# Recurrent feed-forward layer of a small graph network: transposed rows leave PSUM in copies of two tiles instead of four

## The chip, the cores and the metric

The kernel runs on one core of a Trainium2 chip. The metric is the time of one execution on the device, in microseconds (us), taken as the median of several runs. The engines are named as in the profile: PE is TensorE's matmul, PEld its loading of weights, DVE is VectorE, ACT is ScalarE, POOL is GpSimd, SP issues DMAs.

## The reference

The program is two layers over 3327 rows of 256 features: a graph attention, a mixture of 16 experts, a second graph attention and, last, a recurrence. The change is in the recurrence alone. Cut to it, the reference is:

```python
def step(h, _):
    h = h + 0.01 * jnp.tanh(h)
    h = h * jax.nn.sigmoid(h)
    h = _layernorm(h, ln_w, ln_b)
    h = jnp.einsum('bsc,dc->bsd', h, W) + b
    return (h, None)
x, _ = jax.lax.scan(step, x, None, length=N_ITERS)   # N_ITERS = 30
```

The state that the scan starts from is the normalized output of the second attention, and its result is added to that output.

## The kernel before

The rows stand in SBUF as 26 tiles of 128 rows by 256 features in float32, in one tensor `x`. The layers before the recurrence are not touched by the change. They end at 1106 us of the span; the recurrence is the rest.

A step goes over seven groups of tiles: groups 0 to 5 have four tiles each (G = 4), group 6 has two. For one group of n tiles the code issues, in this order:

- ACT: `th` = tanh of the state (L997).
- POOL: `th` = `th` + state (L999); the state is kept scaled by S = 100, which absorbs the factor 0.01.
- ACT: `z` = silu of `th` (L1000).
- DVE: the statistics of `z`, one instruction a tile (L1005), and their combination (L985); POOL: two small instructions that make the inverse deviation `rr` (L987, L988).
- PE: two transposes a tile (L1007) turn `z` into `pt`, a PSUM tile of the pool ps3t with two buffers.
- ACT: one copy of the whole of `pt` into `zT` in SBUF (L1009): 128x1024 for four tiles, 128x512 for the two of group 6.
- PE: two matmuls a tile (L1013) multiply `zT` by the matrix `wc` into `po`, a PSUM tile of the pool ps3o, also with two buffers. The profile shows each of these matmuls as two passes of 128x256: 4 passes a tile, 16 for a group of four tiles, 8 for group 6.
- DVE: the next state from `po`, `rr` and the bias, one instruction a tile (L1018), written into `x`.

So a step has 52 transposes and 104 passes of products. In the last step the group is also added to rows that were kept in DRAM (L1025, after a DMA load, L1024) and written out (L76).

The order of instructions on each engine is not that of the code. The framework's scheduler places them when the program is built, subject to data, to buffers coming free (`th`, `z`, `zT`, `pt` and `po` have two buffers each) and to its own estimates; each engine then works through its list in order and waits on semaphores. On PE the list before has this for a step (counts of instructions; a prime marks the next step):

```
pt x8 group 0, pt x8 group 1 | po x8 group 0, po x8 group 1
pt x8 group 2, pt x8 group 3 | po x8 group 2, po x8 group 3
pt x8 group 4, pt x8 group 5 | po x8 group 4, po x8 group 5
pt x4 group 6, pt x6 group 0' | po x4 group 6
```

The first row of the next step then begins with the two transposes of group 0' that are left. So the groups go in pairs, and group 6 goes by itself.

Of the kernel before, what the change touches and what calls it, by code (L numbers as in the profile page):

```python
# [30 lines left out]
def gat_moe_gat_recurrent_ffn(ctx: ExitStack, tc: tile.TileContext, a: dict, out: bass.AP):  # L31
    nc = tc.nc
# [40 lines left out]
    def move_pairs(dram, tile, c0, c1, into_dram):  # L73

        def move(dst, src):
            nc.sync.dma_start(*((dst, src) if into_dram else (src, dst)))  # L76

        full = min(c1, PAIRS - 1)
        if full > c0:
            move(  # L80
                dram[c0 * 2 * P : full * 2 * P, :].rearrange("(t p b) d -> p t (b d)", p=P, b=2),
                tile[:, : 2 * (full - c0), :].rearrange("p (t b) d -> p t (b d)", b=2),
            )
        if c1 == PAIRS:
            base, last = (PAIRS - 1) * 2 * P, 2 * (PAIRS - 1 - c0)
            for r0, r1 in spread(REST // 2):
                move(
                    dram[base + 2 * r0 : base + 2 * r1, :].rearrange("(p b) d -> p (b d)", b=2),
                    tile[r0:r1, last : last + 2, :].rearrange("p b d -> p (b d)"),
                )  # L90
            if REST % 2:
                move(dram[base + REST - 1 : base + REST, :], tile[REST // 2 : REST // 2 + 1, last, :])
# [882 lines left out]
    with ExitStack() as st:  # L975
        ps_t = st.enter_context(tc.tile_pool(name="ps3t", bufs=2, space=PSUM))
        ps_o = st.enter_context(tc.tile_pool(name="ps3o", bufs=2, space=PSUM))
        last_p = st.enter_context(tc.tile_pool(name="last", bufs=2))

        def inv_norm(stats, n):  # L980


            v = small.tile([P, G, 2], F32, name="v")
            for j in range(n):
                nc.vector.bn_aggr(v[:, j, :], stats[:, j, :])  # L985
            r = small.tile([P, G], F32, name="rr")
            nc.gpsimd.tensor_scalar(r[:, :n], v[:, :n, 1], EPS, None, op0=ALU.add)  # L987
            nc.gpsimd.tensor_tensor(r[:, :n], r[:, :n], neg_half[:, :n], ALU.pow)  # L988
            return r

        for step in range(N_STEPS):
            for ts in groups:
                n = len(ts)
                hs = x[:, ts[0] : ts[0] + n, :]
                th = steps.tile([P, G, D], F32, name="th")
                z = steps.tile([P, G, D], F32, name="z")
                nc.scalar.activation(th[:, :n, :], hs, AF.Tanh, scale=1.0 / S)  # L997

                nc.gpsimd.tensor_tensor(th[:, :n, :], th[:, :n, :], hs, ALU.add)  # L999
                nc.scalar.activation(z[:, :n, :], th[:, :n, :], AF.Silu, scale=1.0 / S)  # L1000
                stats = small.tile([P, G, 6], F32, name="stats")
                pt = ps_t.tile([P, G, KD, P], F32, name="pt")
                zT = steps.tile([P, G, KD, P], F32, name="zT")
                for j in range(n):
                    nc.vector.bn_stats(stats[:, j, :], z[:, j, :])  # L1005
                    for k in range(KD):
                        nc.tensor.transpose(pt[:, j, k, :], z[:, j, k * P : (k + 1) * P], ident)  # L1007
                rr = inv_norm(stats, n)
                nc.scalar.copy(zT[:, :n, :, :], pt[:, :n, :, :])  # L1009
                po = ps_o.tile([P, G, D], F32, name="po")  # L1010
                for j in range(n):
                    for k in range(KD):
                        nc.tensor.matmul(  # L1013
                            po[:, j, :], lhsT=zT[:, j, k, :], rhs=wc[:, k, :],
                            start=(k == 0), stop=(k == KD - 1),
                        )
                for j in range(n):
                    nc.vector.scalar_tensor_tensor(  # L1018
                        x[:, ts[0] + j, :], po[:, j, :], rr[:, j : j + 1], bb, op0=ALU.mult, op1=ALU.add
                    )  # L1020
                if step == N_STEPS - 1:
                    here = slice(ts[0] * P, (ts[-1] + 1) * P)
                    old = last_p.tile([P, G, D], F32, name="old")
                    nc.sync.dma_start(old[:, :n, :], kept[here, :].rearrange("(t p) d -> p t d", p=P))  # L1024
                    nc.vector.scalar_tensor_tensor(  # L1025
                        hs, hs, 1.0 / S, old[:, :n, :], op0=ALU.mult, op1=ALU.add
                    )
                    move_pairs(out, hs, ts[0] // 2, (ts[-1] + 1) // 2, True)
# [49 lines left out]
```

## Time and profile before

| | before |
|---|---|
| median of 7 runs | 2012.43 us (2010.3 to 2014.83) |
| the profiled execution's own time | 2012.6 us |
| span of its profile | 2010.9 us |
| PE busy | 1935.0 us (96%) |
| DVE, ACT, POOL busy | 1299.5 us (65%), 1095.9 us (54%), 952.7 us (47%) |
| granted TensorE clock, mean | 0.993 |
| recurrence in the span | 1106 us to the end |

The profile is of one execution. A busy engine is one with an instruction under way; the instructions of PE overlap, so the distance from one start to the next says more of its rate than the duration of one. An idle time stands beside what ended it. In the timeline, equal instructions that follow each other without a gap are one row with a count.

### The profile page before, as it was taken

The page shows a single profiled execution, that of the slowest core. Times are in us where ns is not written, and L with a number is a line of the kernel's source. Part 1 is how long each engine was busy: PE and PEld are TensorE (multiplying, and loading weights), DVE is VectorE, ACT ScalarE, POOL GpSimd, SP SyncE. Part 2 cuts the span into 40 slices and gives each one's busy share as a digit, 9 for nine tenths or more (in the row PEclk, how much of TensorE's full clock was granted, in tenths as well). Part 3 has the DMA queues.
Part 4 walks back from the last instruction along what each step waited for, and adds up shares of the span by engine and source line. Part 5 has one row for each costly group of instructions (what it writes and reads, how often), then busy time and mean ns, then how long its engine had stood idle before and what let it go on. Part 6 is the DMA issues. An engine that isn't in the chain of part 4 may idle for free.

```text
span 2010.9 us, 33554 instructions
## 1 busy us (share of the span) xinstructions
PE 1935.0 (96%) x12032; PEld 1752.0 (87%) x12032; DVE 1299.5 (65%) x3847; ACT 1095.9 (54%) x1419; POOL 952.7 (47%) x870
## 2 busy tenths in 40 slices
PE   7999999999999987999999999999999999999998
PEld 6999999989999986888888888888888888888887
DVE  6887887722222215667676777777777777777777
ACT  2966766621111114567555666666666666666664
POOL 3020212443333324001000777877887787787785
PEclk9999999999999998999999999999999999999999
DMA  8977141199999854000000000000000000000003
GB/s 165 119 99 117 15 72 49 50 303 321 348 326 310 299 171 137 8 9 16 9 16 11 25 1 1 1 1 1 1 1 1 1 1 1 1 1 1 1 1 115
DMA packets 139755, 157.08 MB, mean 78 GB/s; under 512 B 52028, under 2 KB 99365, under 8 KB 139587
## 3 DMA queue, kind: packets, MB, share of 16 engines
q1 hardware_dynamic: 123466, 122.05, 19.5%
q0 software_dynamic: 11440, 28.09, 8.2%
q10 hardware_dynamic: 4680, 4.76, 0.7%
q8 instruction: 98, 1.61, 0.3%
q14 instruction: 71, 0.57, 0.1%
HBM read 164.58 MB, written 29.78 MB: 97 GB/s over the span
## 4 chain that ended last, share of the span: by engine, by line
PE 68%; issue 10%; POOL 5%; ACT 5%; DVE 4%; DMA 2%; another core or an unknown queue 0%; SPq 0%; POOLq 0%; DVEq 0%; ACTq 0%
PE po L1013 35%; PE acc L262 23%; PE pt L1007 5%; ACT zT L1009 5%; POOL given L831 2%; POOL rb L730 2%; DVE pT L257 2%; PE bank L786 2%; DMA given<-wh,to 2%; PE acc L827 1%; PE bank L499 1%; PE bank L221 1%; DMA zT<-given 0%; POOL rstd L120 0%
## 5 line engine op out<-in xcount | busy, mean ns | idle before, releaser
L1013 PE MATMUL po<-wc,zT 128*128 128x256 f32 x3120 | 706.0, 383 | 21.7 <-ACT zT L1009 21.1
L1013 PEld LDWEIGHTS po<-wc,zT 128*128 128x128 f32 x3120 | 583.4, 190 | 124.5 <-ACT zT L1009 49.9
L262 PE MATMUL acc<-wh,pT 128*128 128x129 f32 (+1 forms) x4056 | 606.4, 310 | 3.2 <-DVE pT L257 3.1
L262 PEld LDWEIGHTS acc<-wh,pT 128*128 128x128 f32 x4056 | 561.2, 191 | 41.4 <-DVE pT L257 4.8
L252 ACT ACTIVATE e<-rb,minus,full 128x384 f32<-128x384 f32 (+3 forms) x494 | 400.2, 824 | 182.0 <-DVE pT L257 163.6
L999 POOL TENSOR_TENSOR th<-th,x 128x1024 f32<-128x1024 f32 (+1 forms) x210 | 460.9, 2215 | 63.9 <-ACT th L997 63.9
L257 DVE SCALAR_TENSOR_TENSOR pT<-e,part,adjT 128x384 f32<-128x384 f32 (+3 forms) x494 | 380.3, 774 | 138.3 <-PE acc L262 120.7
L1018 DVE SCALAR_TENSOR_TENSOR x<-po,rr,bb 128x256 f32<-128x256 f32 x780 | 324.9, 477 | 118.3 <-PE po L1013 113.9
L1009 ACT COPY zT<-pt 128x1024 f32<-128x1024 f32 (+1 forms) x210 | 199.0, 948 | 333.9 <-PE pt L1007 333.9
L1005 DVE BATCH_NORM_STATS2 stats<-z 128x6 f32<-128x256 f32 x780 | 283.7, 415 | 117.5 <-ACT z L1000 117.5
L120 POOL TENSOR_TENSOR rstd<-ve,neg_half 128x4 f32<-128x4 f32 (+3 forms) x28 | 30.0, 1072 | 405.5 <-DVE ve L118 316.0
L988 POOL TENSOR_TENSOR rr<-rr,neg_half 128x4 f32<-128x4 f32 (+1 forms) x210 | 208.0, 990 | 17.4
L1000 ACT ACTIVATE z<-th 128x1024 f32<-128x1024 f32 (+1 forms) x210 | 210.7, 1003 | 0.5 <-POOL th L999 0.5
L997 ACT ACTIVATE th<-x 128x1024 f32<-128x1024 f32 (+1 forms) x210 | 199.4, 996 | 1.9 <-DVE x L127 0.9
L1007 PE MATMUL pt<-ident,z 128*128 128x128 f32 x1560 | 191.0, 274 | 2.5 <-DVE high L943 2.5
L1007 PEld LDWEIGHTS pt<-ident,z 128*128 128x128 f32 x1560 | 178.8, 142 | 14.8 <-issue 2.9
L820 DVE TENSOR_TENSOR pT<-e,bank 128x512 f32<-128x512 f32 x61 | 41.9, 687 | 182.8 <-PE bank L786 122.1
L786 PEld LDWEIGHTS bank<-hT,wh 128*128 128x128 f32 x1280 | 150.7, 194 | 8.1 <-issue 3.4
L786 PE MATMUL bank<-hT,wh 128*128 128x128 f32 x1280 | 151.9, 277 | 5.5 <-issue 3.0
L816 ACT ACTIVATE e<-bank 128x512 f32<-128x512 f32 x61 | 36.4, 597 | 194.6 <-issue 91.3
L831 POOL DMA_INDIRECT given<-wh,to x61 | 60.2, 987 | 167.7 <-DVE wh L830 148.6
L565 POOL DMA_INDIRECT lists<-pair,ati x52 | 62.5, 1202 | 134.7 <-DVE ati L552 44.0
(189 smaller groups left out, 1241.8 us busy)
## 6 DMA issues: line engine op xcount, KB each, us to landing
wh<-in_w_dram SPq DMA_DIRECT2D x120, 512.0 KB
first_set<-in_w_dram SPq DMA_DIRECT2D x63, 512.0 KB
in_bytes<-in_adj_dram POOLq DMA_DIRECT2D x3, 2496.0 KB
x<-in_x_dram SPq DMA_DIRECT2D x6, 512.0 KB
kept<-x SPq DMA_DIRECT2D x8, 384.0 KB
old<-kept SPq DMA_DIRECT2D x6, 512.0 KB
out_dram<-x SPq DMA_DIRECT2D x6, 512.0 KB
table_x<-row ACTq DMA_DIRECT2D x3, 768.0 KB
```

The costliest lines, as they stand in the source:

```text
L252: nc.scalar.activation(e[:, : n * P], rb[:, : n * P], AF.Relu, scale=sc.full[:, j, h : h + 1], bias=sc.minus[:, j, h : h + 1],)
L257: masked = nc.vector.scalar_tensor_tensor(pT[:, : n * P], e[:, : n * P], sc.part[:, j, h : h + 1], adjT[:, j // 2, ts[0] * P : (ts[-1] + 1 ...
L262: nc.tensor.matmul(po[c], lhsT=pT[:, c * P : (c + 1) * P], rhs=wh[:, j, h, :], start=(j == 0 and c % per_bank == 0), stop=(j == NT - 1), s ...
L786: nc.tensor.matmul(p[:, f, :], lhsT=w[:, k, f * P : (f + 1) * P], rhs=hT[:, k, :], start=(k == 0), stop=(k == KD - 1),)
L988: nc.gpsimd.tensor_tensor(r[:, :n], r[:, :n], neg_half[:, :n], ALU.pow)
L999: nc.gpsimd.tensor_tensor(th[:, :n, :], th[:, :n, :], hs, ALU.add)
L1000: nc.scalar.activation(z[:, :n, :], th[:, :n, :], AF.Silu, scale=1.0 / S)
L1005: nc.vector.bn_stats(stats[:, j, :], z[:, j, :])
L1007: nc.tensor.transpose(pt[:, j, k, :], z[:, j, k * P : (k + 1) * P], ident)
L1009: nc.scalar.copy(zT[:, :n, :, :], pt[:, :n, :, :])
L1013: nc.tensor.matmul(po[:, j, :], lhsT=zT[:, j, k, :], rhs=wc[:, k, :], start=(k == 0), stop=(k == KD - 1),)
L1018: nc.vector.scalar_tensor_tensor(x[:, ts[0] + j, :], po[:, j, :], rr[:, j : j + 1], bb, op0=ALU.mult, op1=ALU.add)
```

## The change

```diff
                 rr = inv_norm(stats, n)
-                nc.scalar.copy(zT[:, :n, :, :], pt[:, :n, :, :])
+                for j in range(0, n, 2):
+                    nc.scalar.copy(zT[:, j : j + 2, :, :], pt[:, j : j + 2, :, :])
                 po = ps_o.tile([P, G, D], F32, name="po")
```

A group of four tiles has two copies of 128x512 where it had one of 128x1024; group 6 has one copy of 128x512 as before. Nothing else in the code changes; lines behind the copy move down by one (the copy is L1010, the products L1014, the next state L1019, the last addition L1026).

The scheduler makes other lists of it. In the built program a step on PE now reads:

```
pt x8 group 0, pt x6 group 1 | po x8 group 0
pt x2 group 1, pt x6 group 2 | po x8 group 1
pt x2 group 2, pt x6 group 3 | po x8 group 2
pt x2 group 3, pt x6 group 4 | po x8 group 3
pt x2 group 4, pt x6 group 5 | po x8 group 4
pt x2 group 5, pt x4 group 6 | po x8 group 5, po x4 group 6
```

The products of a group stand in halves of four instructions, each half with a wait of its own for ACT. Of a group's two copies on ACT only the first has a wait for PE. Between two pairs of copies ACT has one `z` and one `th`; behind the last three copies of a step it has the `z` of groups 0 and 1 and the `th` of groups 2 and 3 of the next step.

## The prediction

> **What bounds the kernel now.** I read the page first. PE is busy 96% of the span, and its two costliest lines in the recurrence are the products (L1013) and the transposes (L1007).
>
> ```profile
> PE 1935.0 (96%) x12032; PEld 1752.0 (87%) x12032; DVE 1299.5 (65%) x3847; ACT 1095.9 (54%) x1419; POOL 952.7 (47%) x870
> ...
> L1013 PE MATMUL po<-wc,zT 128*128 128x256 f32 x3120 | 706.0, 383 | 21.7 <-ACT zT L1009 21.1
> ...
> L1009 ACT COPY zT<-pt 128x1024 f32<-128x1024 f32 (+1 forms) x210 | 199.0, 948 | 333.9 <-PE pt L1007 333.9
> ```
>
> The reader is to see that the products' only idle time, 21.7 us, is a wait for the copy, and that ACT in its turn stands idle before the copy until PE has turned the rows. Next, the busy time by stretches (columns: length, then busy time and count of PE, PEld, DVE, ACT and POOL, then the granted clock):
>
> ```profile
> 1106.00:1117.00 11.00, 10.54 (x50) 9.50 (x51) 7.64 (x28) 7.14 (x8) 3.63 (x4) 0.84 0.32 110
> 1117.00:1999.00 882.00, 861.05 (x4606) 748.12 (x4605) 647.74 (x2300) 554.95 (x617) 697.52 (x620) 1.00 0.02 5
> ```
>
> In the steady part PE is busy for 861 of 882 us at a full clock, POOL 698, DVE 648, ACT 555: PE sets the time, and none of the others is near it. Third, the timeline of PE over one step, in order:
>
> ```profile
> 1505.52 1.91 PE L1007 MATMUL pt<-ident,z 128*128 128x128 f32 x16
> 1507.66 7.17 PE L1013 MATMUL po<-wc,zT 128*128 128x256 f32 x32 [0.23 <-ACT zT L1009]
> 1514.67 1.91 PE L1007 MATMUL pt<-ident,z 128*128 128x128 f32 x16
> 1516.81 7.17 PE L1013 MATMUL po<-wc,zT 128*128 128x256 f32 x32 [0.23 <-ACT zT L1009]
> 1523.82 1.25 PE L1007 MATMUL pt<-ident,z 128*128 128x128 f32 x10
> 1525.10 1.99 PE L1013 MATMUL po<-wc,zT 128*128 128x256 f32 x8
> 1526.93 1.25 PE L1007 MATMUL pt<-ident,z 128*128 128x128 f32 x10
> 1528.41 7.17 PE L1013 MATMUL po<-wc,zT 128*128 128x256 f32 x32 [0.23 <-ACT zT L1009]
> 1535.42 1.91 PE L1007 MATMUL pt<-ident,z 128*128 128x128 f32 x16
> ```
>
> A step takes 1535.42 - 1505.52 = 29.90 us. I take it apart by starts. 32 passes of products take 1514.67 - 1507.66 = 7.01 us, 8 passes 1526.93 - 1525.10 = 1.83, so one pass is (7.01 - 1.83) / 24 = 0.2158 us, and 1.83 - 8 x 0.2158 = 0.10 us comes on top once a block. That is the first weight load after a wait: on PEld it starts together with the first pass (1525.10 both) and not ahead of it. A transpose is (1.91 - 1.25) / 6 = 0.11 us. What is left between the transposes and the products is the wait: 2.14 - 16 x 0.11 = 0.38 us twice, 1528.41 - 1526.93 - 10 x 0.11 = 0.38 once more, and 1.28 - 10 x 0.11 = 0.18 at group 6. The sum is 104 x 0.2158 + 52 x 0.11 = 28.16 of work, 3 x 0.38 + 0.18 = 1.32 of waits and 4 x 0.10 = 0.41 (unrounded) of first loads: 29.89. All that the change can touch is the last two, 1.73 us a step.
>
> **What a wait is made of.** The timeline of ACT shows the copies of the same step, the 128x1024 of group 2 and the 128x512 of group 6:
>
> ```profile
> 1506.60 1.01 ACT L1009 COPY zT<-pt 128x1024 f32<-128x1024 f32 x1 [3.43 <-PE pt L1007]
> ...
> 1524.46 0.59 ACT L1009 COPY zT<-pt 128x512 f32<-128x512 f32 x1 [3.42 <-PE pt L1007]
> ```
>
> Group 2's last transpose is over at 1505.52 + 8 x 0.11 = 1506.40; the copy starts 0.20 later, takes 1.01, and the products start 0.05 after its end: 1.26 us, of which the eight transposes of group 3 cover 0.88. Left: 0.38. Group 6's last transpose is over at 1524.26; 0.20 + 0.59 + 0.05 = 0.84, covered by six transposes of the next group, 0.66. Left: 0.18. Both rows repeat in all 29 steady steps.
>
> **The change part by part.** *The stops of PE.* In the changed order of PE the products of groups 0 to 4 each come six transposes after the last transpose of their own group. The first copy is now 128x512. That is exactly the stop of group 6 in the row at 1525.10: same copy, same six transposes, so 0.18 of wait and 0.10 of first load. Group 5 has only the four transposes of group 6 behind it: 0.84 - 0.44 = 0.40 of wait, and 0.10. Group 6's copy runs while the products of group 5 do (16 x 0.2158 = 3.45 us, against two or three copies in a row), so nothing there. The second half of a group's products starts 8 x 0.2158 = 1.73 us after the first, and the second copy ends 0.59 us or less after the first: nothing there either, though behind that added wait stand four products and all that PE has after them. The new sum is 28.16 + 5 x 0.18 + 0.40 + 6 x 0.1035 = 30.08. Against 29.89 that is +0.19 us a step: the waits hardly change (1.30 for 1.32), for there are six short stops in place of three long and one short, and two more first loads. Over 30 steps: +5.6 us.
>
> *The ends of the recurrence.* In the first step before, PE didn't stop (the timeline has pt at 1106.46 and po at 1109.27, at the clock of 0.84, behind a copy that was done at 1108.82). I expect none after either; what is absent is a stop of 0.48 before and of 0.28 after, +0.2. In the last step group 6 was turned with no next group behind it: pt at 2002.22, po at 2003.55, a wait of 0.89 and not 0.18. After, group 6's stop is gone: -0.7. But then the products of group 5 and 6 end only 1.73 us apart, and DVE has both behind them: four L1018 (1.66 in the timeline), one more (0.39, the spacing of the four), the addition for group 5 (1.23), one more (0.40) and that for group 6 (0.69). Counted from the end of PE's last pass it is 0.12 + 0.39 + 1.23 + 0.40 + 0.69 = 2.8 us, where before it was 1.7 (po ends at 2003.55 + 1.99, the last addition at 2006.57 + 0.69): +1.1. The writes to DRAM behind it (SP, 3.6 us to the span's end) come in the same order; I take 0, at most +0.5.
>
> *The copies.* ACT has 180 copies more:
>
> ```profile
> L1000 ACT ACTIVATE z<-th 128x1024 f32<-128x1024 f32 x176 | 187.5, 1065 | 0.0
> ...
> L1009 ACT COPY zT<-pt 128x1024 f32<-128x1024 f32 x178 | 179.4, 1008 | 226.5 <-PE pt L1007 226.5
> ...
> L1009 ACT COPY zT<-pt 128x512 f32<-128x512 f32 x29 | 17.0, 586 | 99.2 <-PE pt L1007 99.2
> ```
>
> 2 x 0.586 - 1.008 = 0.16 us a group, 180 x 0.16 = 29 us of ACT. I cost it at nothing, because ACT is idle when a group's last transpose ends. A group's period on PE is 16 x 0.2158 + 8 x 0.11 + 0.28 = 4.6 us; between two pairs of copies ACT has one `z` (1.07) and one `th` (1.06), with the copies 3.3 us. POOL's own period is 2.37 (L999) + 0.24 (L987) + 1.04 (L988) = 3.65, DVE's 1.66 + 1.40 + 0.36 = 3.4. The tightest place is the turn of the step: three copies, two `z` and two `th`, 1.8 + 2.1 + 2.1 = 6.0 us from the start of the first copy, against 0.84 less 0.20 to the products of group 5, their 3.45, group 6's 1.73, eight transposes 0.88 and 0.20: 6.9. About 1 us of cover. If it goes, every us that ACT is late is a us of PE.
>
> *Sum:* 5.6 + 0.2 - 0.7 + 1.1 = +6.2 us on the profiled execution's 2012.6, 2018.8; the median of the runs stands 0.2 under it, so 2018.6. The unknown with the most leverage is the stop: 150 of them have one row as their pattern, and 0.01 us on it is 1.5 us. Its bounds are the nearest rows: with the longer copy it would be 0.38, and below it cannot go under no wait at all. I keep 0.18, since copy, cover and order are the same and the mean of the 29 copies is 586 ns with a shortest of 585. For what rounding leaves I allow 2 us on both sides: 2016.6 to 2020.6.
>
> A rule that speaks against the change: the Trainium skill, TensorE: Matmul & The Clock Gate, section "A second HAM failure mode: psum-queue depth-cycling", tells of a kernel where PE paused so often between groups of matmuls that its clock swung between half and full rate. By that rule six stops a step might cost up to a second 28.16 us a step, an estimate of 845 us in all. The trace speaks the other way: with four stops a step, up to 0.48 us each, the granted clock is 1.00 over 882 us. I take the row.
>
> **The rivals.** *ACT late (slower, 2033).* At the turn of the step POOL makes `rr` for groups 5, 6 and 0' (1.28 + 0.94 + 1.28 us) between its L999. If the `th` that a `z` needs comes late there, the two copies queued behind that `z` come late, and PE stands. It decides from 1 us of delay on; half a us beyond it, once a step, is +15 us. For it: POOL is the next busiest, 698 of 882 us, and the order is in-order. Against it: 3.65 of 4.6 us. The same with two places is 2048.
>
> *The stops vanish (faster, 1960).* The first copy reads two tiles, four transposes. If it were released by these four alone and not by all eight, ten transposes would cover it (1.10 against 0.84), even the eight behind group 5 (0.88). Then all six stops go, and a step is 28.16: 30 x 1.73 = -52 us. It decides at the point where the cover passes 0.84 us. Against it: the last two transposes of a group stand in the list behind the products of the group before, the second copy has no wait of its own, so the first must wait for the whole group. A smaller form: the first load costs nothing after the new waits, 30.08 - 0.62 = 29.46 a step, -13 us, some 2000; against it, the 0.10 was worked out at just such a short stop.
>
> *No change.* If the stop is 0.15 and not 0.18 (and the tail gives nothing), the sum is about +1 us.
>
> **How the numbers follow.** A measurement of this kernel tells about 0.2%, 4 us, from no change. My forecast, slower by 6 us, has 0.70; ACT late, 0.10; the stops vanish or shrink well, 0.08; no change, 0.12. Of the forecast 0.04 lies under +4 us: faster 0.08, same 0.12 + 0.04 = 0.16, slower 0.66 + 0.10 = 0.76. The range reaches up to 2025, part of the way into ACT late, and down to 2013.5. It leaves out the vanishing stops (0.08), the later half of ACT late (0.06) and half of no change (0.06): 8 in 10.
>
> **What would show it.** After: 150 rows of po with 16 passes behind x8 transposes (x6 and x2 merged), each with a stop of 0.28 by starts; a step of 30.08; 390 copies of 0.59 and none of 1.01; ACT idle before each pair, ended by PE; clock 1.00. The prediction is wrong if a step is under 29.9, if ACT's idle time before the copies is gone, or if PE waits for anything but the copy.

## The result: slower by 0.24%, and the profile after

The changed kernel takes 2017.52 us (median of 15 runs, 2015.58 to 2020.71). The kernel before, now 35 runs, takes 2013.04. The ratio is 1.0024, with a 95% interval of 1.0017 to 1.0031: +4.5 us, with an interval of 3.4 to 6.2. The forecast was 2018.6 against 2012.43, +6.2, at the upper end of that interval.

The page of the changed kernel, the same lines as before:

```profile
PE 1946.4 (97%) x12032; PEld 1746.8 (87%) x12032; DVE 1295.6 (64%) x3847; ACT 1128.4 (56%) x1599; POOL 953.5 (47%) x870
...
L1014 PE MATMUL po<-wc,zT 128*128 128x256 f32 x3120 | 721.5, 385 | 10.3 <-ACT zT L1010 7.2
...
L1010 ACT COPY zT<-pt 128x512 f32<-128x512 f32 x390 | 208.0, 590 | 298.2 <-PE pt L1007 298.1
```

This page is a trap. PE's idle time before the products has halved, 21.7 to 10.3 us, and the kernel is slower. Transposes and products overlap, and a modelled end lies behind the start of the next instruction: a transpose counts as busy for 0.27 us, but the next one starts after 0.11. Of a stop of 0.18 us only 0.02 is left as idle time. What the page lost as idle time, 11.4 us, it shows as busy time of PE, 1935.0 to 1946.4. The idle time of the weight loads, PEld, shows what PE's hides: before the products they waited for the copy 119 times before the change, 49.9 us in all, and 180 times after it, 53.0 us. The starts tell how long each stop is; here is PE's timeline over one step after, where the rows that are left out repeat the ones above them:

```profile
1502.46 3.72 PE L1014 MATMUL po<-wc,zT 128*128 128x256 f32 x16
1506.02 1.04 PE L1007 MATMUL pt<-ident,z 128*128 128x128 f32 x8
1507.08 3.72 PE L1014 MATMUL po<-wc,zT 128*128 128x256 f32 x16
...
1519.86 0.82 PE L1007 MATMUL pt<-ident,z 128*128 128x128 f32 x6
1520.92 5.45 PE L1014 MATMUL po<-wc,zT 128*128 128x256 f32 x24 [0.24 <-ACT zT L1010]
1526.20 1.69 PE L1007 MATMUL pt<-ident,z 128*128 128x128 f32 x14
1527.91 3.72 PE L1014 MATMUL po<-wc,zT 128*128 128x256 f32 x16
1531.47 1.04 PE L1007 MATMUL pt<-ident,z 128*128 128x128 f32 x8
1532.53 2.64 PE L1014 MATMUL po<-wc,zT 128*128 128x256 f32 x11
```

A step is 1532.53 - 1502.46 = 30.07 us, where it was 29.90. Behind eight transposes the products start 1.06 us after the first of them, and 8 x 0.109 is 0.87: a wait of 0.18 (0.183 before rounding), with no idle time written beside it. Then 16 passes take 3.56 where 16 x 0.2158 is 3.45: the first load. Group 5 has six transposes in its row (two of its own, four of group 6) and waits 0.40. ACT, in its timeline, stands idle before every pair of copies until PE is done:

```profile
1501.82 1.07 ACT L1010 COPY zT<-pt 128x512 f32<-128x512 f32 x2 [1.42 <-PE pt L1007]
1502.78 1.07 ACT L1000 ACTIVATE z<-th 128x1024 f32<-128x1024 f32 x1
1503.88 1.06 ACT L997 ACTIVATE th<-x 128x1024 f32<-128x1024 f32 x1
1506.44 1.07 ACT L1010 COPY zT<-pt 128x512 f32<-128x512 f32 x2 [1.49 <-PE pt L1007]
```

### The profile page after: what moved, and what is told of

It reads as the page before. It is cut to its first block, busy times and chain, and to the rows that moved or that the text cites. A ratio compares the mean times of both kernels' runs of the same rounds, so it can differ in the third digit from the quotient of the medians.

```text
span 2014.4 us, 33823 instructions
## 1 busy us (share of the span) xinstructions
PE 1946.4 (97%) x12032; PEld 1746.8 (87%) x12032; DVE 1295.6 (64%) x3847; ACT 1128.4 (56%) x1599; POOL 953.5 (47%) x870
## 4 chain that ended last, share of the span: by engine, by line
PE 70%; issue 10%; POOL 6%; DVE 4%; DMA 3%; ACT 1%; SPq 0%; POOLq 0%; another core or an unknown queue 0%; DVEq 0%; ACTq 0%
PE po L1014 36%; PE acc L262 24%; PE pt L1007 8%; POOL given L831 2%; POOL rb L730 2%; DVE pT L257 2%; DMA given<-wh,to 2%; ACT zT L1010 1%; PE bank L786 1%; PE bank L499 1%; PE bank L221 1%; DMA zT<-given 0%; DMA lists<-pair,ati 0%; POOL rstd L120 0%; PE bank L147 0%
## 5 line engine op out<-in xcount | busy, mean ns | idle before, releaser
L1014 PE MATMUL po<-wc,zT 128*128 128x256 f32 x3120 | 721.5, 385 | 10.3 <-ACT zT L1010 7.2
L1014 PEld LDWEIGHTS po<-wc,zT 128*128 128x128 f32 x3120 | 577.9, 190 | 124.3 <-ACT zT L1010 53.0
L1019 DVE SCALAR_TENSOR_TENSOR x<-po,rr,bb 128x256 f32<-128x256 f32 x780 | 324.9, 477 | 139.5 <-PE po L1014 137.5
L1010 ACT COPY zT<-pt 128x512 f32<-128x512 f32 x390 | 208.0, 590 | 298.2 <-PE pt L1007 298.1
L1005 DVE BATCH_NORM_STATS2 stats<-z 128x6 f32<-128x256 f32 x780 | 277.4, 413 | 103.9 <-ACT z L1000 100.4
L997 ACT ACTIVATE th<-x 128x1024 f32<-128x1024 f32 (+1 forms) x210 | 206.3, 999 | 5.6 <-DVE x L127 0.9
L1007 PE MATMUL pt<-ident,z 128*128 128x128 f32 x1560 | 199.7, 273 | 2.5 <-DVE high L943 2.5
```

Source lines behind the costliest of these rows:

```text
L1010: nc.scalar.copy(zT[:, j : j + 2, :, :], pt[:, j : j + 2, :, :])
L1014: nc.tensor.matmul(po[:, j, :], lhsT=zT[:, j, k, :], rhs=wc[:, k, :], start=(k == 0), stop=(k == KD - 1),)
L1019: nc.vector.scalar_tensor_tensor(x[:, ts[0] + j, :], po[:, j, :], rr[:, j : j + 1], bb, op0=ALU.mult, op1=ALU.add)
```

## The experiments

All but one of the kernels below write the recurrence in the order in which PE is to work, with each PE instruction pinned behind the one ahead of it. So order and copy can be set apart: in the traces PE's list with the changed kernel's order pinned is that of the changed kernel, instruction for instruction, and with the order of before that of the kernel before. The lists of ACT, DVE and POOL are left to the scheduler and differ in places; where that matters it is said. In the steady part PE waits for copies alone, but for the run with four spare copies. In the code `WIDTH` is the number of tiles in a copy, and `ORDER` is "alt6" for the changed kernel's order, "pair" for that of before and "alt8" for a strict alternation; `COVER` counts in "pair" alone.

Three theories stood against each other. *Cover*, that of the prediction: a stop is 0.84 us for a copy of two tiles (1.26 for four) less what PE has to do between a group's last transpose and its products, and 0.10 for the first load. *Alternation*: each change from turning to multiplying costs its 0.28 us by itself. *Copies*: the 180 added copies cost the time. The first four runs shared a chip, on which the kernel before took 2008.14 us, and the last four another, on which it took 2007.49; ratios are to these. The layers ahead of the recurrence end between 1100.0 and 1106.5 us in these traces, so versions from different chips are compared by their steps.

**The new order with the old copy.**

```python
        WIDTH, ORDER, COVER = 4, "alt6", 6
```

> The order of the changed kernel on every engine's list, held fixed, but with the one copy of 128x1024 a group. Cover theory: a stop of PE is 0.20 + copy + 0.05 us less what PE has to do between a group's last transpose and its products, and 0.10 for the first weight load. The copy of 1.01 behind six transposes (0.66) leaves 0.60, behind four 0.82, so a step is 28.16 + 5 x 0.70 + 0.92 = 32.6 us, 2.5 more than with the halves: about 2093. Rival, alternation: each change from turning to multiplying costs its 0.28 us whatever the copy: as the changed kernel, 2017.5. Rival, copies: the 180 added copies cost the 4.5 us: as before, 2013.

Measured: 2089.21 us, ratio 1.0405 (1.0388 to 1.0423), +81 us. PE's timeline:

```profile
1503.71 1.04 PE L1010 MATMUL pt<-ident,z 128*128 128x128 f32 x8
1505.19 3.72 PE L1026 MATMUL po<-wc,zT 128*128 128x256 f32 x16 [0.45 <-ACT zT L1019]
```

The products start 1.48 us after the first of the eight transposes, 0.42 later than with the short copy: the whole difference of the two copies, 1.008 - 0.586. A step is 32.63, 2.56 more than in the changed kernel. The alternation theory falls: as many changes, and 30 x 2.56 = 77 us more. So does the copies theory: fewer copies, and slower.

**The old order with the new copies.**

```python
        WIDTH, ORDER, COVER = 2, "pair", 6
```

> The order of the kernel before on PE, held fixed, but with two copies of 128x512 a group. Cover theory: the pair's second group gives eight transposes of cover (0.88) against 0.84, so the three long stops go and only group 6's 0.28 is left: 28.4 a step, 1.47 less than before: about 1969. Rival, alternation: the order is that of before, so 2013. Rival, copies: 180 copies more, as the changed kernel: 2017.5.

Measured: 1970.27 us, ratio 0.981 (0.9793 to 0.9827), -38 us where cover said -44. PE's timeline:

```profile
1512.09 1.91 PE L1010 MATMUL pt<-ident,z 128*128 128x128 f32 x16
1513.83 7.14 PE L1026 MATMUL po<-wc,zT 128*128 128x256 f32 x32
1520.81 1.91 PE L1010 MATMUL pt<-ident,z 128*128 128x128 f32 x16
```

1513.83 - 1512.09 = 1.74 is 16 x 0.109: the wait is gone. But 32 passes take 6.98 and not 6.91: the copy is ready when the products' turn comes and not earlier (the first weights start to load at 1513.80, 0.03 us ahead of the first pass, where in the next run it is 0.11), and 0.07 of the first load stays. Three times a step that is 0.2 us, 6 us in all, which is what the expectation missed. ACT's list is not quite that of before: it has the four copies of a pair one behind the other, where the kernel before has a `z` between its two. That does not touch the stop, which ends with the pair's first copy. This is the diff's own edit without the new order of PE, and it gains 1.9%: what made the changed kernel slower came with the order.

**Two transposes earlier.** The two transposes of a group that the changed kernel puts behind the products of the group before go ahead of them, and group 6's products go behind the transposes of group 0'; once with the halves, once with the whole copy (`WIDTH` 4).

```python
        WIDTH, ORDER, COVER = 2, "alt8", 6
```

> The changed kernel with the last two transposes of a group moved ahead of the products of the group before; PE goes strictly pt of one group, po of the group before. Cover theory: a group's last transpose now has the whole products of another group (3.45 us) between it and its own products, so no stop is left: 28.15 a step, about 1960, with PE's wait for the copy at 0. Rival, alternation: seven changes a step in place of six, 2026. Rival, copies: 2017.5.

> The same strict alternation with one copy of 128x1024 a group. Cover theory: 1.26 us against 3.45 and more of cover, no stop, 28.15 a step, about 1960, the same as with the halves: the size of the copy no longer matters. Rival, alternation: 2026. Rival, copies: as before, 2013, and 4.5 us below the same order with halves.

Measured: 1956.23 us with the halves, ratio 0.9734 (0.9717 to 0.975); 1958.0 with the whole copy, 0.9749 (0.9733 to 0.9765). The page of the one with halves, and PE's timeline:

```profile
L1026 PE MATMUL po<-wc,zT 128*128 128x256 f32 x3120 | 708.3, 379 | 0.0
```

```profile
1500.17 1.04 PE L1010 MATMUL pt<-ident,z 128*128 128x128 f32 x8
1501.05 3.62 PE L1026 MATMUL po<-wc,zT 128*128 128x256 f32 x16
1504.50 1.04 PE L1010 MATMUL pt<-ident,z 128*128 128x128 f32 x8
```

Products start 0.88 us after the first of eight transposes, transposes 3.45 after the first of 16 passes: no stop and no first load. A step is 28.14 in both, and the intervals overlap: with the products of another group as cover, the size of the copy does not matter. A strict alternation, which has one change a step more than the changed kernel, is the fastest version of all, 30 x 1.93 = 58 us below the changed kernel; only the place of two transposes a group, and of group 6's products, separates them.

**Less cover.** Four transposes of a group ahead of the products of the group before, in place of six; `first` is their number.

```diff
-                first = 2 * g["n"] if ORDER == "alt8" or held is None or len(ts) < G or ts[0] == 0 else 6
+                first = 2 * g["n"] if ORDER == "alt8" or held is None or len(ts) < G or ts[0] == 0 else 4
```

> The changed kernel with all lists as they are but for PE: four transposes in place of six between a group's last transpose and its products, the other four behind the products. Cover theory: the wait grows by 2 x 0.11 to 0.40 at five more stops, 31.2 us a step, about 2051. Alternation theory: as many changes as in the changed kernel, 2017.5.

Measured, in a single run: 2047.5 us, beside 2007.49 for the kernel before. PE's timeline:

```profile
1514.27 1.04 PE L1010 MATMUL pt<-ident,z 128*128 128x128 f32 x8
1515.54 3.72 PE L1026 MATMUL po<-wc,zT 128*128 128x256 f32 x16 [0.24 <-ACT zT L1019]
1519.10 1.04 PE L1010 MATMUL pt<-ident,z 128*128 128x128 f32 x8
```

The page has 42.8 us of idle time before the products (10.3 in the changed kernel), a step is 31.16, and every stop is now 0.40 + 0.10 by starts. Two transposes of cover are worth 2 x 0.11 us at each of the five stops that lost them, as the sum has it. With the run of the new order and the old copy, the wait has been moved by the copy and by the cover separately, and by the expected amount both times.

**A PSUM tile for each half.** This one leaves the order to the scheduler.

```diff
-        ps_t = st.enter_context(tc.tile_pool(name="ps3t", bufs=2, space=PSUM))
+        ps_t = st.enter_context(tc.tile_pool(name="ps3t", bufs=4, space=PSUM))
...
-                pt = ps_t.tile([P, G, KD, P], F32, name="pt")
+                pts = [ps_t.tile([P, 2, KD, P], F32, name="pt") for _ in range(0, n, 2)]
```

> The changed kernel with a PSUM tile of its own for each half of a group (128x512, four buffers), so that a copy is released by the four transposes that it reads. The order is left to the scheduler, which then puts a group's products six transposes behind the last transpose of its first half. Cover theory: cover 0.66 again, so six stops of 0.28 a step, 29.85 us, 0.05 less than before: with the end that alternation brings about 2012 to 2014, no change. Rival (of the prediction): once halves are released by themselves the stops vanish: about 1960.

Measured: 2005.44 us, ratio 0.9994 (0.9984 to 1.0004): no change against the kernel before. PE's timeline:

```profile
1502.21 1.04 PE L1007 MATMUL pt<-ident,z 128*128 128x128 f32 x8
1503.27 3.72 PE L1014 MATMUL po<-wc,zT 128*128 128x256 f32 x16
```

A step is 29.85, with six waits of 0.18. Such a row of eight has the last two transposes of a group's first half, the four of its second half and the first two of the next group, so the products again come six transposes behind the half that they need first. So releasing the first copy by its own four transposes, which this version does, is not enough for the rival "the stops vanish": the scheduler's list moves along with it, and PE stands 0.18 us here as in the changed kernel. That the scheduler takes the copy to be ready that much too early is a guess; what it goes by was not looked into, and the version with own tiles and the changed kernel's order held was not run.

**ACT with more to do.** Copies that nobody reads, one and then four, behind a group's own, in the changed kernel's order.

```diff
+            for _ in range(1):
+                pinned(nc.scalar.copy(last_p.tile([P, KD, D], F32, name="spare"), wc))
```

> The changed kernel's lists with one copy more of 128x512 on ACT, SBUF to SBUF, behind a group's own copies: 210 more, about 0.5 us each by the spacing of the copies, some 100 us of ACT. It reads a constant and nobody reads its result. Hidden theory: ACT's idle time before the next copies is 1.4 to 1.9 us in the changed kernel's timeline, so the added 0.5 (1.0 where the step turns) costs nothing: 2017.5, within 2 us. Rival, ACT's work counts: up to +100 us, and a tenth of it would still show as 10.

> The same with four copies more a group, about 2.0 us, and 4.0 where the step turns. Hidden theory: the idle time of 1.4 to 1.9 us is used up, ACT is late by 0.1 to 0.6 us at a group and by 2.3 at the turn, and PE with it: 3 to 5 us a step, 2110 to 2170; PE's wait for the copy then is longer than 0.18. If ACT's margin were larger than the timeline shows: 2017.5.

Measured with one: 2015.56 us, ratio 1.0038 (1.0024 to 1.0052) to the kernel before. The changed kernel's 1.0024 has 1.0017 to 1.0031, so the two intervals overlap, and the step settles it: 30.07, the same to 0.01 us. ACT's timeline shows the idle time giving way, 1.42 us to 0.98:

```profile
1502.00 1.07 ACT L1019 COPY zT<-pt 128x512 f32<-128x512 f32 x2 [0.98 <-PE pt L1010]
1502.96 0.63 ACT L1021 COPY spare<-wc 128x512 f32<-128x512 f32 x1
1503.48 1.07 ACT L1001 ACTIVATE z<-th 128x1024 f32<-128x1024 f32 x1
```

210 x 0.52 us by the spacing, 109 us of work on ACT, cost nothing, three times what the change itself added to ACT's busy time (32.5 us by the pages). With four the cover is gone: 2183.19 us in a single run, and two steps take 71.7 us, so 5.8 us a step more than in the changed kernel where 3 to 5 were expected. Here the scheduler also changed ACT's list: every second step the `z` of group 1 stands behind four spare copies, and PE's timeline has a long stop there:

```profile
1634.83 1.09 PE L1010 MATMUL pt<-ident,z 128*128 128x128 f32 x8 [0.63 <-ACT z L1001]
1640.71 1.54 PE L1010 MATMUL pt<-ident,z 128*128 128x128 f32 x6 [4.79 <-ACT z L1001]
1642.05 5.53 PE L1028 MATMUL po<-wc,zT 128*128 128x256 f32 x16
1647.42 1.04 PE L1010 MATMUL pt<-ident,z 128*128 128x128 f32 x8
```

Steps of 39.2 and 32.5 us follow in turn. It is a way for ACT to be late at the turn of the step, with its price, but not the one of the rival "ACT late": here PE waits for a `z` that stands late in ACT's list, not for copies behind a `z` that POOL holds up. The changed kernel has 1.4 to 1.9 us of ACT's idle time between it and any such delay.

## Why the prediction was right, point by point

- *PE sets the time, and the stops are all that the change can touch.* Right. With all stops gone a step is 28.14, and the working had 28.16.
- *Six stops of 0.18 + 0.10, and one of these 0.40, in place of three of 0.38 and one of 0.18.* Right: 30.07 measured for 30.08, 29.90 for 29.89. The difference is 0.17 and not 0.19, 29 steady steps of it 4.9 us for 5.6; the rest is rounding: by starts the waits are 0.39 and 0.183, and a transpose takes 0.109 and not 0.11. The bound of 0.38 that the prediction gave for this stop with the longer copy is a misreading: it belongs to eight transposes of cover, and behind six it would be 1.26 - 0.66 = 0.60, as the run with the old copy measured (0.61).
- *The first step, +0.2.* Mis-sized. Before, from pt at 1106.46 to pt at 1116.82 it took 10.36 us where a steady pair takes 9.15, because the clock granted to its 16 transposes was 0.62 (3.01 us for 1.91) and to the products behind them 0.83 up to 1113 us. After, the first step is 30.10 for 30.07: its 14 transposes took 1.72, at a clock of 1.00. So the term was -1.2. That looks like chance at the start and not like the change: with the same list of PE the run with one spare copy took 3.00 us from the first of these 14 transposes to the products, where the changed kernel took 1.74.
- *The last step, -0.7.* About right, -0.65 by the stop of 0.89 that is gone and the last one's 0.46 in place of 0.40.
- *The tail on DVE, +1.1, and the writes, 0 to +0.5.* Right, +1.1 and +0.4. The timeline's end after:

```profile
2005.93 2.21 DVE L1019 SCALAR_TENSOR_TENSOR x<-po,rr,bb 128x256 f32<-128x256 f32 x5 [1.75 <-PE po L1014]
2008.06 1.22 DVE L1026 SCALAR_TENSOR_TENSOR x<-x,old 128x1024 f32<-128x1024 f32 x1
2009.19 0.48 DVE L1019 SCALAR_TENSOR_TENSOR x<-po,rr,bb 128x256 f32<-128x256 f32 x1
...
2009.71 0.69 DVE L1026 SCALAR_TENSOR_TENSOR x<-x,old 128x512 f32<-128x512 f32 x1
```

  Five of L1019, one addition, one more L1019, and the last addition ends at 2010.40, 2.8 us behind PE. The span ends 4.0 us later, where it was 3.6.
- *Sum.* The recurrence takes 2014.4 - 1105.2 = 909.2 us, where it took 2010.9 - 1106.5 = 904.4: +4.8 for +6.2. The medians say +4.5. The first step alone is off by 1.4, as much as the whole miss; the steady steps' 0.7 too much and the writes' 0.4 too little about cancel, with what rounding leaves.
- *The copies at nothing.* Right, and shown by the spare copy. ACT's busy time rose by 32.5 us on the page for the 29 worked out. The cover at the turn of the step was put at about 1 us; the timeline has 1.65 there, and 1.4 to 1.9 elsewhere.
- *The clock.* Right to go by the row. The windows of the changed kernel have 1.00 over the 882 us from 1117 on, with six stops a step. What the Trainium skill tells of another kernel (TensorE: Matmul & The Clock Gate, "A second HAM failure mode: psum-queue depth-cycling") did not come here, with stops of 0.3 to 0.5 us.
- *The rivals.* "ACT late" did not come: ACT is idle before every pair. "The stops vanish" did not come; the working against it, that the first copy waits for the whole group, fits, but own tiles alone don't bring it either. What does is the place of two transposes, which the prediction had in its hands (it named them as the argument against the rival) and didn't follow up. The ten transposes of cover that it counted for the rival leave out that for groups 1 to 5 the products of the group before, 3.45 us, stand between them.

## What to carry to other kernels

Where two engines hand work back and forth, write down for each hand-over its latency (signal, copy, signal) and what the waiting engine has to do in between, from starts; a smaller piece shortens the latency, but a scheduler that places the work anew can take the saved time back by moving the consumer forward, and pay the fixed part of a stop more often. Here putting a whole block of other work between producer and consumer, by order alone, was worth 2.5%, and with it the size of the copy didn't matter. An idle time in a profile with overlapping instructions counts short stops as busy: compare distances between starts.

## What the runs showed of the hardware

- A first pass after a wait costs 0.10 us more than the others (0.320 for 0.216 from start to start), whether the wait is 0.18 us (the changed kernel) or 0.83 (the new order with the old copy); when the data is ready just at the turn, without a wait, 0.07 of it stays (0.286, the old order with the new copies); with the data long there, next to nothing (0.218, two transposes earlier).
- The clock did not fall with the number of short stops, and it did behind long ones. It was 1.00 in the steady part with no stop a step and with six, of up to 0.93 us with the first load (the new order with the old copy). Behind each stop of 4.79 us in the run with four spare copies the granted clock was 0.50 for a while (the mean from 1117 to 1999 us was 0.95): from 1640.71 to 1645.89 us transposes came every 0.213 us for 0.109 and passes every 0.427 for 0.216, and so the 16 passes of the row at 1642.05 took 5.37 us where 3.45 is usual. No steady stop between these lengths was met, so where the limit lies stays open.
- Splitting a copy of 128x1024 (1.008 us) into two of 128x512 costs less than 2 x 0.586: back to back they take 1.07 together, for the second starts 0.48 us after the first, before that has ended.
